# A planner's smaller TensorE grant for background work in each step, and another place where the attention sums' tile is allocated

## The chip, the cores and the metric

The kernel runs on one core of a Trainium2 chip. The metric is device time in microseconds of one execution; the time of a kernel is the median of its runs. Engine names in the profile: PE is TensorE's matmuls and PEld its weight loads, DVE is VectorE, ACT is ScalarE, POOL is GpSimd, SP is SyncE, which here only issues DMAs.

## The reference

Input x is 8 images of 256 channels by 32 x 32 pixels, all in float32. Two layers follow each other.

Layer 0 normalises x in groups of channels and adds an attention over the image:

```
q = q_w . x                                  8 heads of 32, 1024 queries
k_map, v_map = kv_w . x                      256 channels each
pooled(t): for sides 32, 16, 11, 5: average-pool t, add its 3x3 depthwise convolution
k, v = layernorm(pooled(k_map)), layernorm(pooled(v_map))     1426 keys
att = softmax(q . k / sqrt(32)) . v
out = proj_w . (att mixed within each head) + proj_b
x = x + out
```

Layer 1 takes the 1024 pixels of an image as tokens: layer norm, an attention over 256 channels with one head, then a layer norm and a mixture of eight dense experts of three matrices each, weighted by a gate that is a softmax over the mean of all images. Both parts are added to their input.

## The kernel before, in words

**A planner writes the order.** No engine decides at run time what to do next. While the program is built, the class `Flow` (line 665) keeps a modelled clock for every engine (`now`), and for every tile the modelled time at which it is written and read (`ready`, `read`). Each instruction goes through `note` (line 786), which prices it with `cost` (line 744), advances the engine's clock, and ties it behind the last instruction of its engine. The order in which the builder emits instructions is thus the order in which each engine runs them.

**Foreground.** `attention` (line 954) walks through a list of 360 steps (`steps`, line 2124): for each of 8 images b, for the two channel halves c (four heads each), for two halves of the queries (512), for eleven chunks of 128 keys; one more step for each image computes the scores of the last 25 keys of all four combinations together ("tail", at the ninth place of the image). A step emits `scores` (line 1650): four matmuls of 32 rows in a tile sc of four PSUM banks, of which there is one, and ScalarE's exponential into a tile pt. Then, for the chunk of the step before, `values` (line 1660): four matmuls of 32 columns that accumulate into pv. After the last chunk of a combination, `tail_values` adds the tail's part, and ScalarE copies pv to the tile att (line 2177), which is allocated once for each (b, c) (line 2144) in one of two buffers.

**Background.** All other work is written as generators, called threads, that yield what they need next: an engine, the tiles that have to be there, and a PSUM tag. `spawn` sorts them by rank. Rank 0: the sums of the probabilities (`unit`, `sums`), the normalisation, the reading back of queries. Rank 1: `project` (line 1767), which multiplies att by a matrix in four chunks and adds the result in DRAM, with a buffer xr between; also the pooling by halves (`halve`) and the start of the small convolutions. Rank 2: `value_tokens` and `key_tokens`, which transpose the convolved maps by groups of four and layer-norm them. Rank 4: `prepare` (line 1500), the next image's load, its statistics, the four maps (`maps`, line 1227, three chunks each: 512, 512 and 146 pixels) and its queries (`queries`, line 1549, four chunks, written to DRAM and read back). The convolution's taps on VectorE (`convolve`, line 1394) have rank 7. Layer 1 has ranks 5 and 6 (`outputs`, `layer1`, `norm`). I call the work of ranks 0 to 4 preparation for short, and the TensorE work between two yields of a thread a chunk.

**How much of it goes between two steps.** After each step the loop calls `f.step((PACE, PACE1))` (line 2179). `step` (line 923) adds PACE = 4.0 us of planned TensorE time to the credit of ranks under 5 and PACE1 = 2.0 to that of ranks from 5 up (`FILLER`), each held to 1.5 times its pace (`CAP`), and then resumes threads in the order of rank as long as one is runnable; what a thread spends on TensorE is taken from its credit (line 921), which can go below zero. For TensorE a thread is runnable (lines 902 to 911) when its inputs are planned to be there 1.5 us before `until`, a PSUM buffer is free by then, and

```
until = max(pe, self.free("sc") - 0.5)
(self.credit[rank >= FILLER] > 0 or pe < until - 0.5)
```

that is, when there is credit, or when TensorE's modelled clock pe is over 0.5 us before the time at which sc comes free for the next scores. The call in the middle of a step (line 2155), without a pace, is closed to TensorE.

**Due times.** `finish` (line 936) is the other way in which threads run: the loop calls it where it can't go on without something, and it resumes whichever thread can start first, with the credit set to 1.0, until the condition holds. The places are the key tokens of the image (line 2140, before chunks 0, 4 and 8, and line 2150 before the tail), its queries (line 2142), a free pt (line 2153), the value tokens (line 2164), and at the end of a combination the projection of the image before (line 2176). The maps run ahead within limits: `maps` waits for free map buffers and for earlier maps to be convolved, and an image's fourth map needs the value tokens of that image, which wait for the image before it to be in attention.

**After the loop** the rest of layer 1 runs down, and `experts` (line 2323) fills TensorE to the end; parts of it start while layer 1 still runs.

All operations of `Flow` are recorded at line 678, so the profile's groups are told apart by tiles: sc and pv are the foreground; kvw marks maps, qw queries, mt the projection, con with acc, sacc or kt the transposes of tokens, pt with con the sums; y, p, v, t, gw, wv, res and diag belong to layer 1; bank and y with t, h and s3e to the experts.

Of the kernel before, what the change touches and what calls it, by code (L numbers as in the profile page):

```python
# [16 lines left out]
P = 128  # L17
C = 256
HW = 1024
# [9 lines left out]
SCALE0 = DH ** -0.5  # L29
SCALE1 = C ** -0.5  # L30
FILLER = 5
PACE = 4.0
PACE1 = 2.0
CAP = (1.5, 1.5)
NEVER = 1e9
# [918 lines left out]
def attention(tc, kit, f, outer, ended, nb, consts, x, t1, t2, hn, bounds, vecs, q_t, kv_t, proj_t, gqk_t, wqk, wqkv, vecs1, w1_d, w1c, gate_d, wrc, vecs2, bnvec, w2_d, h2d, between, pre, held):  # L954
# [6 lines left out]
    with ExitStack() as ctx:  # L961
        l1, shared = outer
        wp = ctx.enter_context(tc.tile_pool(name="w0", bufs=1))
        work = ctx.enter_context(tc.tile_pool(name="work0", bufs=1))
        psum = ctx.enter_context(tc.tile_pool(name="psum0", bufs=1, space=PSUM))

        def T(pool, shape, tag, bufs=1):
            return f.tile(pool, shape, tag, bufs=bufs)
# [681 lines left out]
        def scores(b, c, sl, kc):  # L1650
            k0, w = KEY_CHUNKS[kc]
            t = T(psum, [P, 4, 512], "sc")
            for j in range(4):
                r = slice(DH * j, DH * j + DH)
                f.pe.matmul(t[:w, j, :], lhsT=ks[b, c][r, k0 : k0 + w], rhs=qs[b, c][r, sl], start=True, stop=True)
            pt = T(work, [P, 4, 512], "pt", bufs=6)
            f.act.activation(pt[:w], t[:w], AF.Exp, scale=SCALE0)
            return pt

        def values(b, c, kc, pt, pv):  # L1660
            w = KEY_CHUNKS[kc][1]
            for j in range(4):
                h = 4 * c + j
                f.pe.matmul(
                    pv[DH * j : DH * j + DH, :],
                    lhsT=vts[b][kc // 4][:w, kc % 4, h * DH : (h + 1) * DH],
                    rhs=pt[:w, j, :],
                    start=kc == 0,
                    stop=False,
                )  # L1670

        def tail_scores(b):
            t = T(psum, [P, 4, 512], "sc")
            for j in range(4):
                r = slice(DH * j, DH * j + DH)
                for u in range(4):
                    c, half = divmod(u, 2)
                    f.pe.matmul(
                        t[DH * u : DH * u + DH, j, :],
                        lhsT=ks[b, c][r, NK - DH :],  # L1680
                        rhs=qs[b, c][r, half * 512 : half * 512 + 512],
                        start=True,
                        stop=True,
                    )
            f.act.activation(ptail, t, AF.Exp, scale=SCALE0)

        def tail_values(b, u, pv):
            for j in range(4):
                f.pe.matmul(
                    pv[DH * j : DH * j + DH, :],  # L1690
                    lhsT=vz[b % 2][DH * u : DH * u + DH, DH * j : DH * j + DH],
                    rhs=ptail[DH * u : DH * u + DH, j, :],
                    start=False,
                    stop=True,
                )

        def tail_add(u, into):
            rows = slice(DH * (u + 1) - NT, DH * (u + 1))
            f.pool.dma_start(
                out=into[:NT].rearrange("p j q -> p (j q)"),  # L1700
                in_=ptail[rows].rearrange("p j q -> p (j q)"),
                accum_op=ALU.add,
            )

        def add(kc, pt, into):

            w = KEY_CHUNKS[kc][1]
            f.pool.dma_start(
                out=into[:w].rearrange("p j q -> p (j q)"), in_=pt[:w].rearrange("p j q -> p (j q)"), accum_op=ALU.add
            )  # L1710
# [120 lines left out]
        projected, taken, written, probabilities = [0], [0], [0], []  # L1831
# [276 lines left out]
        def unit(b, c, sl, n, pairs):  # L2108
            total = yield from sums(n, pairs)
            yield from normalise(b, c, sl, total, n)  # L2110

        atts = {}
# [22 lines left out]
        for i in range(len(steps) + 1):  # L2135
            if i < len(steps):
                b, c, half, kc = steps[i]
                sl = slice(half * 512, half * 512 + 512)
                if kc % 4 == 0:
                    f.finish(lambda: key_parts[0] > 3 * b + kc // 4)  # L2140
                if (half, kc) == (0, 0):
                    f.finish(lambda: (b, c) in qs and (b or (c, 0) in asked))
                    turn[0] = 2 * b + c
                    atts[b, c] = T(work, [P, HW], "att", bufs=2)
                if kc == NKC // 2 and b < nb - 1:
                    f.sp.dma_start(t1[b][:, c, sl], x[b, c * P : (c + 1) * P, sl])
                if b == 0 and kc == 0:
                    f.finish(lambda: (c, half) in asked)
                if kc == NKC - 1:
                    f.finish(lambda: key_parts[0] > 3 * b + 2 and (b, 1) in qs and (b or len(asked) == 4))  # L2150
                    tail_scores(b)
                else:
                    f.finish(lambda: f.vacant("pt"))
                    pts[i] = scores(b, c, sl, kc)
                f.step()
            if i and steps[i - 1][3] < NKC - 1:
                b1, c1, half1, kc1 = steps[i - 1]
                if kc1 == 0:
                    pv = T(psum, [P, 512], "pv")
                    pairs = []  # L2160
                    sl1 = slice(half1 * 512, half1 * 512 + 512)
                    f.spawn(unit(b1, c1, sl1, units, pairs), 0)
                    units += 1
                f.finish(lambda: kc1 // 4 in vts[b1])
                values(b1, c1, kc1, pts[i - 1], pv)
                spent[0] += kc1 == 3
                if kc1 % 2:
                    f.drop(pts[i - 1])
                    add(kc1, pts.pop(i - 1), pts[i - 2])
                    pairs.append(pts.pop(i - 2))  # L2170
                if kc1 == NKC - 2:
                    u = 2 * c1 + half1
                    tail_values(b1, u, pv)
                    pairs.append(pts.pop(i - 1))
                    tail_add(u, pairs[-1])
                    f.finish(lambda: projected[0] >= b1)
                    f.act.activation(atts[b1, c1][:, sl1], pv, AF.Copy)
            if i < len(steps):
                f.step((PACE, PACE1))
        f.columns, f.keep = False, None  # L2180
# [536 lines left out]
def tile_conv_attn_hybrid(  # L2717
# [45 lines left out]
    with tc.tile_pool(name="between", bufs=1) as between, ExitStack() as early:  # L2763
        l1 = early.enter_context(tc.tile_pool(name="l1", bufs=1, side="right"))
        shared = early.enter_context(tc.tile_pool(name="psum_l1", bufs=1, space=PSUM, side="right"))
        f = Flow(tc, kit)

        ended, pre, held = [0], set(), {"w": {}, "todo": []}
        attention(
            tc, kit, f, (l1, shared), ended, nb,  # L2770
            consts, x, t1, t2, hn, bounds, vecs0, q_t, kv_t, proj_t, gqk_t, wqk, wqkv, vecs1, w1_d, w1c, gate_d, wrc, vecs2, bnvec,
            w2_d, h2d, between, pre, held,
        )
        last(f, (l1, shared), ended, early, pre, held)
# [122 lines left out]
```

## Time and profile before

| | us |
|---|---|
| median of three runs | 3174.4 (3173.14 to 3174.69) |
| the profiled execution | 3177.97 |
| its span, first to last instruction | 3176.1 |
| attention loop, by the first scores and the last | 83 to 1825 |
| rest of layer 1 and experts | 1825 to 3176 |

The profile's first part gives each engine's busy time, its share of the span and the number of its instructions. A table by window gives, after the window's limits and length, the busy time of PE, PEld, DVE, ACT and POOL with their instruction counts, then the granted TensorE clock as a share of full speed, the busy share of the DMA engines and the GB/s moved. A list of waits gives who waited for whom, the sum, the number of times and the longest. The timeline gives start, length, engine, operation, tiles, shapes and the number of merged instructions, and in brackets the idle time ahead of it with what ended it. A matmul's length is modelled: the next may start before it is over, so chunks are best measured from start to start. Matmuls of float32 appear twice as often as they are written, and a wide one in four column tiles four times that.

### The profile page before, as it was taken

How to read it: one execution, taken by the hardware profiler on the slowest of the kernel's cores; microseconds unless marked ns; L12 is line 12 of the kernel's file. 1: busy time of each engine (PE TensorE's matmuls, PEld its weight loads, DVE VectorE, ACT ScalarE, POOL GpSimd, SP SyncE). 2: the span in 40 equal slices, each digit the busy share in tenths (PEclk: the TensorE clock that was granted, in tenths of full speed). 3: DMA queues.
4: the chain of work that ended last, by engine and by line, in shares of the span. 5: the costliest groups of instructions: out<-in, count | busy, mean ns of one | idle time of the engine just before them, and what ended most of it. 6: DMA issues, size and time to landing. Idle time of an engine off the chain costs nothing.

```text
span 3176.1 us, 56426 instructions
## 1 busy us (share of the span) xinstructions
PE 3052.5 (96%) x22778; PEld 1794.2 (56%) x22778; DVE 2284.5 (72%) x3823; ACT 1627.8 (51%) x2175; POOL 1287.8 (41%) x1387
## 2 busy tenths in 40 slices
PE   7898899999999999989999999999999999999998
PEld 3332233434434334434433376768888888888887
DVE  6865785995887877877444444558888877777776
ACT  3766666566576576675565523343333344444443
POOL 3423241332332332331221202038566667777776
PEclk9899999999999999999999999999999999999999
DMA  1366855766666666666776725244344310000000
GB/s 55 80 155 142 183 107 116 174 132 128 155 138 138 138 140 142 143 146 134 180 149 131 179 68 202 91 164 148 139 144 149 108 39 21 22 32 21 21 14 22
DMA packets 114223, 364.40 MB, mean 115 GB/s; under 512 B 13904, under 2 KB 40056, under 8 KB 90496
## 3 DMA queue, kind: packets, MB, share of 16 engines
q0 software_dynamic: 28608, 181.68, 29.5%
q1 hardware_dynamic: 81840, 177.02, 16.6%
q8 instruction: 182, 2.98, 0.4%
q10 hardware_dynamic: 3504, 1.99, 0.2%
q14 instruction: 89, 0.73, 0.1%
HBM read 112.99 MB, written 80.26 MB: 61 GB/s over the span
## 4 chain that ended last, share of the span: by engine, by line
PE 70%; DVE 8%; issue 3%; ACT 3%; DMA 3%; POOL 2%; SPq 0%; DVEq 0%; POOLq 0%; ACTq 0%
PE bank L678 21%; PE sm L678 16%; PE y L678 10%; PE sc L678 8%; PE sx L678 7%; PE pv L678 7%; DVE acc L678 2%; ACT pt L678 2%; DMA pt<-pt 2%; DVE pt L678 1%; DVE h L678 1%; DVE u L678 1%; DVE c L678 1%; DMA xi<-in_x_dram 1%; ACT h L678 0%
## 5 line engine op out<-in xcount | busy, mean ns | idle before, releaser
L678 ACT ACTIVATE pt<-sc 128x2048 f32<-128x2048 f32 (+1 forms) x352 | 660.6, 1877 | 310.7 <-PE sc L678 257.0
L678 PE MATMUL sc<-q,kn 32*128 32x512 f32 (+2 forms) x3072 | 417.9, 649 | 49.4 <-ACT pt L678 48.2
L678 DVE TENSOR_TENSOR pt<-pt,pt 128x1024 f32<-128x1024 f32 x280 | 340.6, 1261 | 113.9 <-DMA pt<-pt 111.1
L678 PE MATMUL pv<-pt,vt 128*32 128x512 f32 (+1 forms) x2816 | 379.4, 611 | 0.2 <-ACT att L678 0.2
L678 ACT ACTIVATE h<-h,bnvec 128x512 f32<-128x512 f32 x454 | 343.4, 805 | 65.8 <-DVE h L678 55.6
L678 ACT ACTIVATE p1c<-bank 128x256 f32<-128x256 f32 x227 | 86.8, 382 | 559.0 <-PE bank L678 553.1
L678 DVE SCALAR_TENSOR_TENSOR acc<-map,vec,acc 128x961 f32<-128x961 f32 (+1 forms) x240 | 316.4, 1322 | 31.3 <-ACT acc L678 25.5
L678 POOL TENSOR_TENSOR rstd<-rstd,mhalf 128x4 f32<-128x4 f32 (+2 forms) x88 | 109.9, 1250 | 560.4 <-DVE rstd L678 470.2
L678 POOL DMA_DIRECT2D pt<-pt x160 | 147.1, 920 | 405.0 <-ACT pt L678 319.6
L678 DVE TENSOR_TENSOR h<-p1c,bank 128x512 f32<-128x512 f32 x227 | 154.7, 682 | 201.6 <-PE bank L678 198.5
L678 POOL TENSOR_TENSOR tm<-h,tm 128x256 f32<-128x256 f32 x212 | 242.8, 1145 | 16.6
L678 PEld LDWEIGHTS sc<-q,kn 32*128 32x128 f32 (+2 forms) x3072 | 113.0, 178 | 224.0 <-ACT pt L678 118.8
L678 DVE TENSOR_TENSOR h<-u,bank 128x256 f32<-128x256 f32 x454 | 231.3, 550 | 7.8
L678 POOL TENSOR_TENSOR tm<-h 128x512 f32<-128x512 f32 x106 | 140.1, 1321 | 200.1 <-ACT h L678 198.0
L678 PEld LDWEIGHTS pv<-pt,vt 128*32 128x32 f32 (+1 forms) x2816 | 55.8, 108 | 272.2 <-issue 259.7
L678 DVE SCALAR_TENSOR_TENSOR sacc<-small,vec,sacc 128x480 f32<-128x480 f32 (+8 forms) x384 | 194.8, 515 | 14.9 <-ACT sacc L678 4.7
L678 DVE TENSOR_TENSOR h<-h,gate 128x1024 f32<-128x1024 f32 x128 | 202.4, 1581 | 0.5 <-ACT h L678 0.5
L678 PE MATMUL y<-t,s3e 128*128 128x256 f32 x768 | 187.0, 379 | 3.1 <-POOL t L678 1.8
L678 POOL TENSOR_TENSOR t<-h,t 128x256 f32<-128x256 f32 x218 | 173.8, 797 | 17.1
L678 POOL TENSOR_TENSOR t<-h 128x512 f32<-128x512 f32 x109 | 141.4, 1297 | 94.8 <-DVE h L678 74.1
L678 PE MATMUL bank<-t,s1e 128*128 128x256 f32 x726 | 177.6, 381 | 0.0
L678 DVE TENSOR_TENSOR u<-h,bank 128x512 f32<-128x512 f32 x227 | 156.1, 688 | 25.1 <-PE bank L678 0.8
(374 smaller groups left out, 5663.0 us busy)
## 6 DMA issues: line engine op xcount, KB each, us to landing
pt<-pt POOLq DMA_DIRECT2D x160, 1024.0 KB, 7.8
h<-h SPq DMA_DIRECT2D x111, 512.0 KB
xi<-in_x_dram SPq DMA_DIRECT2D x16, 512.0 KB
t<-t SPq DMA_DIRECT2D x8, 1024.0 KB
res<-t SPq DMA_DIRECT2D x32, 256.0 KB
t<-res SPq DMA_DIRECT2D x32, 256.0 KB
hn<-res SPq DMA_DIRECT2D x32, 256.0 KB
hn<-hn SPq DMA_DIRECT2D x16, 512.0 KB
```

The lines of the kernel that those rows point to most:

```text
L678: ins = fn(*args, **kwargs)
```

## The change

Two things. The grant of ranks under 5 goes from 4.0 to 1.2 us a step (its upper limit from 6.0 to 1.8 with it); the grant of layer 1 stays. And the tile of the sums is allocated just before it is first written, at the end of a combination's first half, where it was allocated at the start of the half of the heads, eleven steps earlier; the `finish` for the projection of the image before moves ahead of it, and so ahead of the tail's values and its addition.

```diff
-PACE = 4.0
+PACE = 1.2
 PACE1 = 2.0
 CAP = (1.5, 1.5)
...
                 if (half, kc) == (0, 0):
                     f.finish(lambda: (b, c) in qs and (b or (c, 0) in asked))
                     turn[0] = 2 * b + c
-                    atts[b, c] = T(work, [P, HW], "att", bufs=2)
...
                 if kc1 == NKC - 2:
+                    f.finish(lambda: projected[0] >= b1)
+                    if half1 == 0:
+                        atts[b1, c1] = T(work, [P, HW], "att", bufs=2)
                     u = 2 * c1 + half1
                     tail_values(b1, u, pv)
                     pairs.append(pts.pop(i - 1))
                     tail_add(u, pairs[-1])
-                    f.finish(lambda: projected[0] >= b1)
                     f.act.activation(atts[b1, c1][:, sl1], pv, AF.Copy)
```

## The prediction

> **What bounds the kernel now.** I read the page's busy shares first, then the busy times by window with the windows cut where each image's attention begins, then the list of waits for TensorE, and last TensorE's timeline at two places.
>
> ```profile
> PE 3052.5 (96%) x22778; PEld 1794.2 (56%) x22778; DVE 2284.5 (72%) x3823; ACT 1627.8 (51%) x2175; POOL 1287.8 (41%) x1387
> ```
>
> TensorE is busy 96% of the span. No other engine is near it, so time is TensorE's work plus its gaps, and a change of order can win back gaps only.
>
> ```profile
> 83.00:308.00 225.00, 200.48 (x1736) 72.06 (x1736) 163.94 (x325) 153.78 (x200) 79.23 (x96) 0.95 0.56 125
> 308.00:517.00 209.00, 193.40 (x1878) 71.87 (x1882) 156.03 (x265) 136.33 (x162) 64.61 (x74) 0.98 0.67 144
> ...
> 1193.00:1405.00 212.00, 202.56 (x1916) 83.00 (x1912) 175.75 (x314) 138.24 (x165) 67.19 (x80) 1.00 0.70 150
> ...
> 1625.00:1825.00 200.00, 197.77 (x2210) 73.23 (x2206) 91.22 (x151) 110.97 (x99) 36.39 (x40) 1.00 0.71 150
> 1825.00:3176.00 1351.00, 1328.68 (x5908) 1111.04 (x5904) 970.61 (x1445) 493.08 (x814) 759.32 (x761) 1.00 0.24 83
> ```
>
> The second number is the window's length, the third TensorE's busy time. The eight attention windows (83 to 1825 us) leave 81 us idle in all: 24.5 in the first image, 15.6 in the second, 12.0, 5.7, 8.4, 9.4, 3.8 and 2.2 after that. The diff touches only this stretch; what follows 1825 us is TensorE-bound at 98% and only shifts.
>
> ```profile
> PE sc L678 <- ACT pt L678: 48.2, 63, 3.0
> PE sm L678 <- DVE mv L678: 15.8, 2, 10.3
> ```
>
> 48.2 us in 63 waits: the scores of a step (sc) wait for ScalarE's exponential of the step before (pt), since sc has one buffer. By window it is 15.0, 6.8, 5.4, 4.9, 3.8, 8.1, 2.1 and 2.0. Of the other row 10.3 us lie before the loop.
>
> ```profile
> 1122.79 1.06 PE L678 MATMUL pv<-pt,vt 128*32 128x512 f32 x8
> 1123.67 1.90 PE L678 MATMUL sm<-xi,kvw 128*32 128x512 f32 x16
> 1125.39 1.90 PE L678 MATMUL sx<-xi,kvw 128*32 128x512 f32 x16
> 1127.11 0.68 PE L678 MATMUL sm<-xl,kvw 128*32 128x146 f32 x16
> 1127.61 1.90 PE L678 MATMUL sm<-xi,kvw 128*32 128x512 f32 x16
> 1129.32 1.90 PE L678 MATMUL sx<-xi,kvw 128*32 128x512 f32 x16
> 1131.15 1.14 PE L678 MATMUL sc<-q,kn 32*128 32x512 f32 x8
> ```
>
> ```profile
> 1370.31 1.14 PE L678 MATMUL sc<-q,kn 32*128 32x512 f32 x8
> 1371.38 1.06 PE L678 MATMUL pv<-pt,vt 128*32 128x512 f32 x8
> 1373.45 1.14 PE L678 MATMUL sc<-q,kn 32*128 32x512 f32 x8 [1.00 <-ACT pt L678]
> 1374.52 1.06 PE L678 MATMUL pv<-pt,vt 128*32 128x512 f32 x8
> 1376.64 1.14 PE L678 MATMUL sc<-q,kn 32*128 32x512 f32 x8 [1.05 <-ACT pt L678]
> ```
>
> The first is a burst: five chunks of the next image's preparation inside one step (9.4 us from scores to scores). The second is starved: scores, values, nothing else, and about 1.05 us of waiting. A step has a floor of 3.14 us, set by ScalarE, of which TensorE's own part is 2.07; with one chunk (1.72 us, start to start) it is 3.79 with no wait. So a step wants at least 1.07 us of other work. Bursts spend in one step what later steps lack.
>
> **What the Trainium skill says.** "TensorE: Matmul & The Clock Gate", Part 2 (step by step): matmuls stay in program order, only weight loads are pulled ahead. So the order the planner writes down is the order that runs; the trace agrees where TensorE waits 1.05 us with more chunks a few steps on. The same page, Part 1: the clock falls after an idle window of about 3.4 us. The trace grants 0.95 in the first image, where waits are most, and 1.00 in the windows from 1193 us. "TensorEngine Tiling (Array Packing)", Key Properties: changing the tiling mode drains the engine. The trace agrees: from values (128x32 tiles) to a chunk in the same tiles is 0.88 us (1122.79 to 1123.67), to untiled transposes 0.99 us elsewhere.
>
> **The change, part by part.**
>
> *PACE 4.0 to 1.2.* In each step the threads of ranks 0 to 4 (sums, projection, tokens, maps, queries) get 1.2 us of planned TensorE time instead of 4.0, at most 1.8 in hand instead of 6.0. No instruction is added or removed. What they need: from the timeline, sorted by tiles and summed start to start, they take 72 us in the first image, 48 in the second, 43 to 44 in each of the next four: about 0.96 us a step over 45 steps. In the planner's own prices (lines 753 to 758 and 813) an ordinary image is 15.8 for maps, 6.9 queries, 6.9 projection, 3.5 sums, 12.8 for eighteen groups of transposes with their mode switch, 0.8 statistics: 46.7, or 1.04 a step against 1.2. So the grant holds the mean. It isn't a hard limit either: line 908 lets a thread run without credit while the planner sees TensorE free over 0.5 us ahead of `until`. After the values of an ordinary step the planner stands about 1.0 us past the scores' end and `until` (line 904: sc free at 0.15 + 1.87 + 0.15, less 0.5) at 1.67, so one chunk goes in whatever the credit. Preparation then runs at one large chunk, or one to two small ones, per step, where it had up to four or five.
>
> What that wins: bursts of 5.5 to 8.3 us come once or twice an image. Spread at one chunk a step, each reaches four to six steps on. Starved steps lie there in part: after the burst at 1339 us come nine waits between 1364 and 1397, six of them of about a microsecond, of which the spread reaches the first two or three. By image: in the first, 15.0 us of waits less two single long ones (3.0 and 2.8) leaves 9, and the work at hand is plentiful; I take two thirds, **6 us**. In the second to sixth, 6.8 + 5.4 + 4.9 + 3.8 + 8.1 = 29.0; I take a third, **10 us**. In the last two, nothing. Ends for this part: 0, if what is spread meets only full steps, and 38 (all of the 9 and the 29).
>
> What it costs: transposes that shared a step fall in separate ones; each extra change of tiling costs 0.11 us in and about as much out; ten more make **2 us** (0 to 8). The layer-1 threads (ranks 5 up) keep 2.0 a step, one chunk of 1.72, so their rate per step stands; if the freed slot goes to preparation first they lose at most the second chunk that some steps have, and it is done after 1825 us at the same price.
>
> What is late next: maps come up to six steps later, and VectorE's convolution with them. In the fifth image the last key tokens were transposed at 913 us and are due at the tail step, 1021: 108 us spare, or over 20 steps. Queries of the second image were written at 218 us and are due at 308: 90 us, 18 steps; there the first image's 72 us against a grant of 55 leaves 17 us, 14 steps' worth, so it just holds. DMAs that move: query writes (256 KB) and the next image's load behind them on SP, whose queue already waits 311.6 us for the query tiles; nothing on SP waits longer for the loop than those 18 steps allow. On POOL the halving (1.28 us a piece) comes between the additions of pt in smaller lots, which is no loss: 0.
>
> *The sums' tile allocated at evacuation, and `finish` moved ahead of the tail's values.* The tile has two buffers; its first write already came after the projection of the last image, by line 2176. Allocation issues no instruction: 0. `finish` emits something only when the projection is late. In the fifth image the projection's four chunks ran between 985 and 1013 us, in the fifth to ninth step, and the check comes at the twelfth; rank 1 keeps them near one a step. If late, TensorE would have the remaining chunks ahead of the tail's values (1.06 us), and behind those wait the copy of the sums on ScalarE and POOL's tail addition; each chunk waits for its buffer's write, 4.8 us to land. Ends: 0 to 20 us an image; I take 0.
>
> **Sum.** 6 + 10 - 2 = 14 us. The profiled execution took 3178.0 us (span 3176.1 and 1.9 around it), so 3164.0 for it; it lies 3.6 above the median 3174.4, which gives 3160.
>
> **Rivals.**
> A, the forecast: part of the starved steps filled, 8 to 24 us won, 3150 to 3166, likeliest 3160. Chance 0.50.
> B, preparation becomes a steady background that is at hand in nearly every starved step: 30 of the 38 us, and 4 to 6 us more from the clock in the first image (5% of 225 us is 11, half of it): 3140. For it: 45 steps and 40-odd chunks an image. Against: the convolution gates the maps, so preparation is not always at hand. Chance 0.17.
> C, the change doesn't do what it says: the rule of line 908 gave one chunk a step before and gives it now, gates of VectorE decide when chunks come; 3174. For it: many steps before had no preparation although credit was 4.0. Against: the bursts are there. Chance 0.13.
> D, slower: preparation falls behind its due step, and `finish` (lines 2140 to 2150) forces it while scores stand. Its price is the missing convolution: eight taps of 1.32 us for a map, 10.6 us, at each of four or five image starts, 42 to 53 us, less half of the 14 won and some of the wait covered by layer 1: about +16, 3190. It decides once preparation is over 18 steps late in the second image or 20 later. For it: the first image needs 1.57 us a step and gets 1.2, unused credit over 1.8 is lost, and the debt carries on. Against: the free chunk, and 90 to 108 us of slack. Chance 0.20.
>
> **Numbers.** A measurement of this kernel can tell about 0.2% (6.3 us) from no change. A falls below 3168 nearly always; faster 0.66 (A 0.49, B 0.17), same 0.14, slower 0.20. The range for 8 in 10 leaves out half of B below and half of D above: 3140 to 3188.
>
> **What would show it.** Right: the waits of sc for pt fall from 48.2 us to 30 to 36; steps with four map chunks are gone; the 98% stretch begins 10 to 20 us earlier than 1825 and keeps its length of 1351. D would show as waits over 5 us for VectorE (acc, kt, sacc) or for q at an image's start. C would show the same bursts. The prediction is wrong if the gain comes from after 1825, or if more than ten such waits stand in the loop.

## The result, and the profile after

The changed kernel took 3157.28 us (median of four runs, 3155.23 to 3158.89), against 3174.55 us for the kernel before (3173.14 to 3176.05): a ratio of 0.9945, 95% interval 0.9928 to 0.9962, or 17 us less. The profiled execution took 3158.89 us, with a span of 3157.0 against 3176.1.

The busy line of the page after:

```profile
PE 3054.6 (97%) x22768; PEld 1796.5 (57%) x22768; DVE 2277.6 (72%) x3824; ACT 1630.0 (52%) x2176; POOL 1286.5 (41%) x1393
```

TensorE's work is what it was (3052.5 before, +2.1), so the whole gain shows as idle time of TensorE: 3176.1 - 3052.5 = 123.6 us before, 3157.0 - 3054.6 = 102.4 after, 21.2 less. 21.2 - 2.1 = 19.1 is the difference of the two spans. Where this idle time was is seen when each trace is cut at its last scores. Limits, length and TensorE's busy time, then clock, DMA share and GB/s; first the kernel before:

```profile
83.00:1817.66 1734.66, 1652.95 (x16602) 0.99 0.66 142
1817.66:3176.10 1358.44, 1336.02 (x6004) 1.00 0.24 84
```

and after:

```profile
83.00:1808.84 1725.84, 1664.63 (x16656) 0.99 0.66 142
1808.84:3157.00 1348.16, 1326.62 (x5944) 1.00 0.24 82
```

The loop's idle time goes from 1734.66 - 1652.95 = 81.7 us to 61.2, that is 20.5 of the 21.2. The stretch after it idles 22.4 and 21.5. Yet the loop is only 8.9 us shorter, and the stretch after it 10.2: in the loop TensorE was busy 11.7 us longer, with 54 matmuls more, and after it 9.4 us less, with 60 fewer. Layer-1 work moved from the end into the loop. So a gap won back in the loop shows up partly as an earlier end of the loop, partly as layer-1 work done earlier. The granted clock was lower as well, 0.989 over the whole profiled execution against 0.991 in the one before, which makes some 6 us more lost at most (an estimate: what is missing to 1, times the span). The 2.3 us that TensorE was busy longer beyond the moved work can be its doing; no run isolates it.

By image, from its first scores to those of the next:

| image | 1 | 2 | 3 | 4 | 5 | 6 | 7 | 8 |
|---|---|---|---|---|---|---|---|---|
| TensorE idle, before | 25.9 | 14.2 | 12.0 | 5.7 | 8.4 | 9.5 | 3.8 | 2.2 |
| after | 19.3 | 10.4 | 4.6 | 10.5 | 5.3 | 2.5 | 7.9 | 0.7 |
| of it sc waiting for pt, before | 15.8 | 6.1 | 5.4 | 4.9 | 3.8 | 8.1 | 2.1 | 2.0 |
| after | 7.8 | 6.1 | 3.1 | 7.0 | 5.1 | 2.1 | 3.7 | 0.6 |

In this count six images win, the fourth and the seventh lose. TensorE's waits in the loop after, with sum, number and longest:

```profile
PE sc L678 <- ACT pt L678: 35.5, 49, 2.8
...
PE sm L678 <- DMA res<-in_w_dram: 4.7, 1, 4.7
PE sx L678 <- DVE acc L678: 3.9, 1, 3.9
```

The scores' waits fell by 48.2 - 35.5 = 12.7 us. The other waits in the loop fell too, by about 8 us; most of them are single ones of up to 5.5 us.

**The bursts are gone.** In the timeline before, the fifth image had five chunks of maps and queries between two scores, at 1122.79 to 1131.15 us. Steps with more than 5 us of preparation, measured start to start, were 13 in the loop before and are 2 after. After, the three chunks of a map lie in three successive steps, with layer-1 products beside them:

```profile
1128.26 1.92 PE L678 MATMUL sm<-xi,kvw 128*32 128x512 f32 x16
1130.01 1.04 PE L678 MATMUL sm<-diag,con 128*32 128x512 f32 x8
1130.98 1.14 PE L678 MATMUL sc<-q,kn 32*128 32x512 f32 x8
1132.05 1.07 PE L678 MATMUL pv<-pt,vt 128*32 128x512 f32 x8
1132.93 1.90 PE L678 MATMUL sx<-xi,kvw 128*32 128x512 f32 x16
1134.65 3.64 PE L678 MATMUL sm<-wv,t 128*32 128x256 f32 x64
1138.21 1.14 PE L678 MATMUL sc<-q,kn 32*128 32x512 f32 x8
1139.28 1.06 PE L678 MATMUL pv<-pt,vt 128*32 128x512 f32 x8
1140.17 0.68 PE L678 MATMUL sx<-xl,kvw 128*32 128x146 f32 x16
```

**A third of the starved steps is gone.** By length alone (scores to scores in under 3.25 us) the short steps are hardly fewer, 59 before and 58 after; but a short step can hold a small chunk. Steps with nothing but scores and values in them, the prediction's sense of starved, are 29 before and 19 after, and waits of about one microsecond before scores (0.9 to 1.15 us) fell from 29 to 15.

The longer of the two heavy steps left is at the twelfth step of the second image, where `finish` now stands ahead of the tail's values:

```profile
341.73 1.90 PE L678 MATMUL sm<-att,mt 128*32 128x512 f32 x16
343.45 1.90 PE L678 MATMUL sx<-xi,kvw 128*32 128x512 f32 x16
345.17 0.68 PE L678 MATMUL sm<-xl,kvw 128*32 128x146 f32 x16
345.67 1.90 PE L678 MATMUL sm<-att,mt 128*32 128x512 f32 x16
347.50 0.33 PE L678 MATMUL sx<-con,acc 128*128 128x128 f32 x1
351.71 0.55 PE L678 MATMUL sx<-con,acc 128*128 128x128 f32 x3 [3.89 <-DVE acc L678]
...
354.85 1.93 PE L678 MATMUL pv<-ptail,vz 32*32 32x512 f32 x8
356.71 2.09 PE L678 MATMUL sc<-q,kn 32*128 32x512 f32 x8
```

Two chunks of the projection (att with mt) were late and stand ahead of the tail's values; `finish` resumes whichever thread can start first, and so two chunks of a map come with them, and transposes that wait 3.89 us for the convolution (acc). Only then come the tail's values and the next scores: the step lasts 16.9 us (339.8 to 356.7).

### The profile page after: what moved, and what is told of

Same layout as the page of the kernel before. It is cut to its first block, busy times and chain, and to the rows that moved or that the text cites. A ratio compares the mean times of both kernels' runs of the same rounds, so it can differ in the third digit from the quotient of the medians.

```text
span 3157.0 us, 56376 instructions
## 1 busy us (share of the span) xinstructions
PE 3054.6 (97%) x22768; PEld 1796.5 (57%) x22768; DVE 2277.6 (72%) x3824; ACT 1630.0 (52%) x2176; POOL 1286.5 (41%) x1393
## 4 chain that ended last, share of the span: by engine, by line
PE 80%; DVE 8%; ACT 4%; issue 4%; DMA 2%; POOL 2%; ACTq 0%; DVEq 0%; POOLq 0%
PE bank L678 22%; PE sm L678 20%; PE y L678 11%; PE sc L678 10%; PE sx L678 9%; PE pv L678 9%; ACT pt L678 3%; DVE acc L678 3%; DMA pt<-pt 2%; DVE h L678 1%; DVE pt L678 1%; DVE u L678 1%; DVE c L678 1%; DMA res<-in_w_dram 1%; ACT h L678 0%
## 5 line engine op out<-in xcount | busy, mean ns | idle before, releaser
L678 PE MATMUL sc<-q,kn 32*128 32x512 f32 (+2 forms) x3072 | 417.9, 645 | 37.1 <-ACT pt L678 35.5
L678 DVE TENSOR_TENSOR pt<-pt,pt 128x1024 f32<-128x1024 f32 x280 | 347.6, 1285 | 137.0 <-DMA pt<-pt 118.5
L678 DVE SCALAR_TENSOR_TENSOR acc<-map,vec,acc 128x961 f32<-128x961 f32 (+1 forms) x240 | 307.4, 1283 | 13.4 <-ACT acc L678 7.8
L678 PE MATMUL sm<-y,t 128*32 128x256 f32 (+1 forms) x2112 | 175.2, 379 | 0.0
```

The costliest lines, as they stand in the source:

```text
L678: ins = fn(*args, **kwargs)
```

## The experiments

All are the changed kernel with one edit. Ratios are to the kernel before, with 95% intervals. The theory at the start: the smaller grant keeps chunks for steps that otherwise lack them, and the second part is worth nothing. Its rivals: the gain is the second part's, or the gain is an accident of the order that the planner happens to write.

**The second part alone.**

```diff
-PACE = 1.2
+PACE = 4.0
```

> Only the second part of the change: the sums' tile at its evacuation and the finish ahead of the tail, the grant still 4.0. Theory 1 (the smaller grant spreads bursts over starved steps, the second part is neutral): 3171 to 3178 us, the scores' wait for the exponential near 48 us, as before. Theory 2 (the later allocation or the earlier finish does it): 3155 to 3162. Theory 3 (any change of order moves the time by some 10 us either way, whatever it is for): anywhere from 3160 to 3190, and the scores' wait doesn't go with the time.

Measured: 3187.7 us, 1.0035 (1.0021 to 1.0049): slower by 13 us than the same grant with the old place. TensorE's order is that of the kernel before, instruction for instruction, until the twelfth step of the second image. There the kernel before has

```profile
365.28 1.06 PE L678 MATMUL pv<-pt,vt 121*32 121x512 f32 x8
366.27 1.06 PE L678 MATMUL pv<-ptail,vz 32*32 32x512 f32 x8
367.26 1.92 PE L678 MATMUL sx<-att,mt 128*32 128x512 f32 x16
369.12 0.65 PE L678 MATMUL sm<-con,kt 128*128 128x128 f32 x4
```

and this one

```profile
363.82 1.07 PE L678 MATMUL pv<-pt,vt 121*32 121x512 f32 x8
364.70 1.90 PE L678 MATMUL sx<-att,mt 128*32 128x512 f32 x16
366.54 0.66 PE L678 MATMUL sm<-con,kt 128*128 128x128 f32 x4
367.13 1.06 PE L678 MATMUL pv<-ptail,vz 32*32 32x512 f32 x8
```

Two chunks changed places with the tail's values. On the spot that cost 0.8 us: this step and the next take 10.36 us here and 9.53 in the kernel before. But from there every modelled clock differs, the planner makes other choices, and at the end the kernel is 13 us slower, with 63.5 us of waits of sc for pt against 48.2. Most of the added waits lie in the rest of this same image: 18.9 us in the second image against 6.1. So at a grant of 4.0 the second part gains nothing, and it can't be the gain by itself; and a difference of 13 us can follow from a displacement that on the spot costs 0.8. That made the third account, accident, a serious one, and the next runs look at the grant at many values.

**The grant at other values**, with the allocation at its new place.

```diff
-PACE = 1.2
+PACE = 2.0
```

> The change with a grant of 2.0 in place of 1.2: up to 3.0 us in hand, so two large chunks in a row are still possible. Theory 1: part of the gain, 3160 to 3168 us, the scores' wait between 36 and 45 us. Theory 3: no order between 4.0, 2.0 and 1.2.

Measured: 3155.24 us, 0.9934 (0.9918 to 0.9949).

```diff
-PACE = 1.2
+PACE = 1.4
```

> The change with a grant of 1.4. Run 1 (second part alone, 13 us slower by moving two chunks once) says that a small change of order can shift the whole plan after it, so single paces scatter by some 10 us; the question is whether the low grants lie together under the high ones. Theory 1 (a small grant wins by spreading): 3150 to 3164 us. Theory 3 (scatter alone): 3155 to 3190, no side taken.

Measured: 3161.03 us, 0.9955 (0.9941 to 0.997).

```diff
-PACE = 1.2
+PACE = 1.6
```

> The change with a grant of 1.6. Theory 1: 3150 to 3166 us, beside 1.2, 1.4 and 2.0. Theory 3: 3155 to 3190, no side taken.

Measured: 3168.99 us, 0.9984 (0.9977 to 0.9991).

```diff
-PACE = 1.2
+PACE = 3.0
```

> The change with a grant of 3.0 (4.5 in hand, bursts of two to three large chunks). The second part emits nothing different at this grant. Theory 1: with the high grants, 3170 to 3190 us, the scores' wait for the exponential above 45 us. Theory 3: 3155 to 3190, no side taken.

Measured: 3197.74 us, 1.0071 (1.0043 to 1.0099).

```diff
-PACE = 1.2
+PACE = 5.0
```

> The change with a grant of 5.0, larger bursts than before. Theory 1: 3172 to 3192 us, the scores' wait 48 us or more. Theory 3: 3155 to 3190, no side taken.

Measured: 3181.45 us, 1.0025 (1.001 to 1.0039).

At 2.0, 3.0 and 5.0 TensorE's order is the same with the allocation at its old place, instruction for instruction, since `finish` then has nothing left to force; so these three are runs of the grant alone. What follows: there is no smooth curve. The four grants from 1.2 to 2.0 took 3155 to 3169 us, their mean is 3160.6; the three from 3.0 to 5.0 took 3181 to 3198, mean 3189.0; the kernel before (4.0 with the old place), 3174.6, is faster than these three. The two groups don't overlap, so the smaller grant is very likely a cause, worth some 28 us between the means at the new place. But inside a group neighbours differ by 4 to 14 us without an order in them, which no account of mine predicts: that is the scatter of the orders. Pure accident is unlikely: of the 35 ways to choose four of the seven kernels, only one puts the four fastest at the four smallest grants. The exact size of 17 us isn't explained by the grant alone.

**The grant under the need.**

```diff
-PACE = 1.2
+PACE = 0.8
```

> The change with a grant of 0.8, under the mean need of 0.96 to 1.04 a step. Theory 1: the free chunk still gives one chunk a step when TensorE would wait, so nothing collapses: 3152 to 3165 us, the scores' wait 30 to 38 us; no forced waits over 5 us at the starts of images. Rival (a grant under the mean makes preparation late and finish forces it): 3175 to 3200, with waits for acc, kt or q.

Measured: 3245.87 us, 1.0219 (1.0202 to 1.0237). The list of waits alone hardly shows why:

```profile
PE sc L678 <- ACT pt L678: 54.6, 56, 3.8
...
PE sc L678 <- DMA q<-hn: 7.0, 1, 7.0
```

The rest is in the groups of TensorE's instructions, among products of a constant with a constant:

```profile
L678 PE MATMUL sm<-con 128*128 128x256 f32 x188 | 41.8, 381 | 0.0
L678 PE MATMUL sx<-con 128*128 128x256 f32 x42 | 9.4, 379 | 0.0
```

These compute nothing that is used: `warm` (line 847) writes such filler wherever the planner sees TensorE wait over 1.8 us, to keep it busy. With others like them in the tiling of the values (128x32) they are 61 us in the loop, 9.0 in the kernel before, and they count as busy. The two groups shown stand mostly at the starts of images, at 295 to 308 us (14 us) and 6 to 7 us each at 754, 999, 1232, 1458 and 1698 us. That is rival D's place and mechanism: preparation comes too late and the next image waits for it. The loop ends at 1914 us, 105 us later than after.

```diff
-PACE = 1.2
+PACE = 1.0
```

> The change with a grant of 1.0, between the change (3157) and 0.8 (3246). The mean need is 0.96 us a step as measured and 1.04 in the planner's prices. If the edge is where the grant no longer covers the need: 3175 to 3215 us, with forced work at the starts of images and filler products. If the free chunk covers a small deficit: 3155 to 3170.

Measured: 3181.85 us, 1.0021 (1.0012 to 1.003). So the edge lies between 1.0 and 1.2. At 1.0 the filler is only 9.7 us; there is one wait for the queries (5.1 us), and the scores' waits are 50.3 us. The longest of these names ScalarE, but ScalarE had stood behind the evacuation of a map, which waited for VectorE's convolution:

```profile
364.66 0.60 ACT L678 ACTIVATE map<-sm 128x512 f32<-128x512 f32 x1 [9.82 <-DVE acc L678]
365.16 0.77 ACT L678 ACTIVATE acc<-sm,vec,mid 128x512 f32<-128x512 f32 x1
365.82 1.88 ACT L678 ACTIVATE pt<-sc 128x2048 f32<-128x2048 f32 x1
```

TensorE's next scores come at 367.75 us, after 7.43 us of waiting. A step of 16.1 us stands shortly before (339.86 to 355.96); in it, late chunks of the projection and chunks of maps stand together before the tail's values. That is late preparation, as rival D has it, though its due point is the projection.

**The free chunk of line 908**, which preparation may run without credit, taken away from it.

```diff
-                and (self.credit[rank >= FILLER] > 0 or pe < until - 0.5)
+                and (self.credit[rank >= FILLER] > 0 or rank >= FILLER and pe < until - 0.5)
```

> The change, but a thread of ranks 0 to 4 no longer runs without credit when TensorE would wait. Theory 1: starved steps with preparation at hand but credit in debt go unfilled, and the first image (1.57 us a step needed, 1.2 granted) falls behind: the scores' wait 48 us or more, 3170 to 3190 us. Rival (the credit alone does the spreading, the free chunk is rarely used): 3154 to 3162, as the change.

Measured: 3182.8 us, 1.0024 (1.0017 to 1.0031), with this wait:

```profile
PE sc L678 <- ACT pt L678: 67.2, 66, 4.8
```

35.5 us with the rule, 67.2 without, and 25.5 us more time, beyond the 4 to 14 by which neighbours differ: at a grant of 1.2 there is no gain without the rule. By the code it is what lets a chunk into an otherwise starved step when the credit is spent; steps with nothing but scores and values are 28 here, 19 with the rule.

**The limit on what may be in hand**, apart from the grant. With 5.0 times 1.2 it is 6.0 us, as it was in the kernel before.

```diff
-CAP = (1.5, 1.5)
+CAP = (5.0, 1.5)
```

> The change with the same mean grant of 1.2, but up to 6.0 us of unused credit in hand (5 times the pace instead of 1.5), as much as before the change. Theory 1a (what counts is that bursts are cut): bursts come back after every stretch in which preparation had no work, 3168 to 3185 us. Theory 1b (what counts is the mean, which keeps preparation spread over the image): 3152 to 3165. Loop idle plus filler products, which went with the time in all runs so far, 70 to 80 us under 1b and 85 to 95 under 1a.

Measured: 3150.57 us, 0.9918 (0.9905 to 0.993), the fastest of the study. Its interval touches that of the change (0.9928 to 0.9962), so it is as fast or a little faster. Some bursts come back in it: seven steps have over 5 us of preparation, against two with the change and 13 before. Yet steps with nothing but scores and values are 16, fewer than with the change. So seven bursts in the loop don't cost the time, against the picture that my prediction had; what counts is the grant per step. Why is argued only: the grant sets how soon after a burst the next chunks follow. Changes of tiling, from the values' tiles to untiled ones, are 95 in this loop against 107.

```diff
-PACE = 1.2
+PACE = 1.0
-CAP = (1.5, 1.5)
+CAP = (5.0, 1.5)
```

> The grant is 1.0 us a step, and 5.0 us may be in hand (1.5 with the limit at 1.5 times the grant, which took 3181.9). Theory L, lost credit: 1.0 is near enough to the mean need (0.96 by the timeline, 1.04 in the planner's prices), and 1.0 failed because what a step left unused beyond 1.5 was lost; with 5.0 in hand nothing is lost, and the time is that of the grant of 1.2, 3148 to 3164, with the waits of sc for pt at 38 to 46 us. Rival theory G, the grant: 1.0 is below what the planner charges, preparation runs late whatever may be in hand, and a wait for the queries or filler products at the images' starts stay: 3174 to 3190.

Measured: 3178.62 us, 1.0013 (1.0006 to 1.002). So lost credit isn't why 1.0 fails, and the grant is, as theory G had it. The change of tiling just counted comes 129 times in this loop, and the scores wait 54.9 us for pt. Of the marks that G named the filler is there (16.9 us in the loop), the wait for the queries isn't.

**How long ahead of the scores a thread must be ready.** If the planner were too careful in letting threads in, a smaller margin would fill more steps.

```diff
-MARGIN = 1.5
+MARGIN = 1.0
```

> The change, and a thread may take TensorE when its inputs are planned to be there 1.0 us ahead, not 1.5. In the order of instructions it leaves about 8 us less room unfilled between values and scores than the change. Theory 1 (time follows the unfilled room of the loop): 3143 to 3153 us, the scores' wait under 32 us. Rival (inputs come later than planned and TensorE waits for them instead): 3155 to 3170, with the scores' wait lower and the other waits higher by as much.

Measured: 3161.07 us, 0.9957 (0.9945 to 0.9969): no gain over the change, against my expectation. The loop's idle time is nearly the same (59.2 us against 61.2). Starved steps are only 11 here, but waits of the scores of over 1.15 us sum to 14.6 us against 9.5.

**One account for all runs.** For each I summed TensorE's gaps in the timeline between 83 us and its last scores (all those before sc, whatever was waited for, and the rest) and the time of the filler in the same stretch:

| kernel | median us | gaps before sc | other gaps | filler | sum | span less sum |
|---|---|---|---|---|---|---|
| limit 5.0 times | 3150.6 | 45.1 | 12.8 | 12.0 | 69.9 | 3078.9 |
| grant 2.0 | 3155.2 | 53.8 | 10.8 | 8.9 | 73.5 | 3081.4 |
| the change (1.2) | 3157.3 | 37.1 | 24.0 | 8.5 | 69.6 | 3087.4 |
| 1.4 | 3161.0 | 46.9 | 17.9 | 15.0 | 79.8 | 3077.1 |
| margin 1.0 | 3161.1 | 40.2 | 18.7 | 6.5 | 65.4 | 3094.4 |
| 1.6 | 3169.0 | 54.6 | 21.1 | 5.4 | 81.1 | 3090.0 |
| before (4.0) | 3174.6 | 49.5 | 32.1 | 9.0 | 90.6 | 3085.5 |
| 1.0, limit 5.0 times | 3178.6 | 56.6 | 16.6 | 16.9 | 90.1 | 3081.5 |
| 5.0 | 3181.5 | 54.0 | 25.0 | 12.4 | 91.4 | 3089.0 |
| 1.0 | 3181.9 | 59.4 | 16.4 | 9.7 | 85.5 | 3094.4 |
| no free chunk | 3182.8 | 70.5 | 12.7 | 6.9 | 90.1 | 3089.3 |
| 4.0, new place | 3187.7 | 66.3 | 20.9 | 10.1 | 97.3 | 3088.9 |
| 3.0 | 3197.7 | 72.3 | 20.6 | 11.0 | 103.9 | 3093.0 |
| 0.8 | 3245.9 | 64.2 | 19.1 | 61.1 | 144.4 | 3107.3 |

Without the last row the spans cover 48 us (3148.8 to 3196.9) and what is left after the sum covers 17 (3077.1 to 3094.4). So most of what tells the kernels apart is idle and filler time in the loop; of the rest, some is the granted clock (below, what stays open). No single column does it: the grant of 2.0 has more waits of sc than the kernel before, and wins by its other gaps; the 0.8 loses by filler.

The count of starved steps (nothing but scores and values) parts them more clearly. It is 11 to 26 in the six kernels up to 3169 us, and 29 to 37 in the kernel before and at 3.0, 4.0 and 5.0. So a grant of 3.0 or more goes with more starved steps, as the prediction had it. A grant of 1.0 or less fails in another way: with 21 to 24 starved steps the two kernels at 1.0 and the one at 0.8 have 20 to 32 us in waits of the scores of over 1.15 us, against 9.5 to 18 in the six.

## Why the prediction was right, and where it wasn't

The time was forecast at 3160 and is 3157.3; rival A's case came true. Point by point:

- **TensorE bound, only gaps to win: held.** Busy +2.1, idle -21.2.
- **Sum of 14 us for the profiled execution: 19.1 measured.** The first image's 6 is 8.0 by the scores' waits (15.8 to 7.8) and 6.6 by all idle time. The 10 us of the second to sixth image were mis-sized as I counted them: the scores' waits there went from 28.3 to 23.4 only, 4.9 won. But the other waits in the same images fell by 11.6 (idle 49.8 to 33.3, less the 4.9), and I had given those no gain at all. The total came out near because one term was too large and one left out; that is luck. The last two images, set at nothing, lost 2.6. If filler is counted as waiting, the place was wrong as well: it was 9.1 us in the first two images before and 1.0 after, and none against 7.4 in the fourth and fifth. Idle time and filler together fell by 18.5 us in the first two images, where my terms hold 8.3 (6, and a third of the second image's 6.8), and by 5.3 in the third to sixth, where they hold 7.4.
- **Two us for ten more changes of tiling: near in number, not shown in time.** They went from 100 to 107 in the loop. TensorE's busy time rose by 2.1, but that can't be put down to them, since the lower granted clock alone is worth some 6 us (the estimate above).
- **Waits of sc for pt to 30 to 36 us: held, 35.5.** Steps with four map chunks: gone. Starved steps went from 29 to 19, near the third that I took. As a cause the burst is weaker than I made it: with the limit at 5.0 times there are seven bursts again, but starved steps are 16 and the time is no worse. What counts is a grant per step between the mean need and twice that (1.2 to 2.0), together with the free chunk (without it 3182.8). The step that isn't borne out is "bursts spend in one step what later steps lack".
- **"Their rate per step stands; keeps its length of 1351": failed.** The stretch after the loop began 8.9 us earlier, not 10 to 20, and was 10.2 us shorter, with 9.4 us less work for TensorE. By my own sign of being wrong, a gain from after the loop, half of the time won counts against me; of the idle time won 20.5 us of 21.2 lie in the loop. I had taken the credit as what holds layer 1 back; line 908 lets it, too, run beyond its credit where a step has room, and steps freed of a burst have. That this is the reason is read from the code; no run isolates it.
- **The second part at 0: failed as a claim, though small on the spot.** `finish` did force chunks in the second image; I had looked at the fifth only. In the changed kernel they cost a step of 16.9 us with 3.9 of waiting in it, inside my bound of 0 to 20. Alone, at 4.0, the second part made the kernel 13 us slower by what followed from it.
- **Rival D: its mechanism is real, its point lies elsewhere.** At 1.2 it doesn't decide: only one wait of 3.9 us for acc, none for q. At 0.8 it does, and at 1.0 in part (the 7.43 us behind the convolution, the 5.1 for the queries). My need of 1.04 in the planner's prices and 0.96 in the trace lie where the edge is, between 1.0 and 1.2; the debt of the first image carried on less than I feared; that the free chunk pays it is argued, not isolated.
- **Rival B's clock: not seen.** The first image was granted 0.93 after, 0.95 before (see the last section).
- **Rival C: out.** The bursts did go, and the grants from 1.2 to 2.0 are all faster than those from 3.0 to 5.0.

What stays open: why one grant inside a group is 4 to 14 us better than its neighbour. The runs show that a displacement of two chunks is enough for 13 us, not by which chain of choices. So of the 17 us the direction is explained by the grant; how much is its mean effect and how much the luck of this order can't be told from one order. The grant of 1.2 with the allocation at its old place was not tried.

A part of the scatter is the granted clock. Of 25 executions of the kernel before, measured together, one with a mean clock of 0.988 took 3181.1 us, and three with 0.994 took 3172.9 to 3173.6. What is missing to 1, times the span, is an estimate of what the clock took at most. On the mean it is 29.2 us for the change, 24.6 to 27.4 for the kernel before, 17.0 for the limit at 5.0 times, and 31.9 for the second part alone. So the gain of the change isn't the clock's. The lead of the limit at 5.0 times over the change (6.7 us) can be, and so can up to 7 of the 13 us that the second part alone lost. Between the groups it is 25.8 us at the four small grants and 30.0 at the three large ones, 4 of the 28 us. Whether a kernel's order or chance sets its clock is not shown.

## What to carry to other kernels

When a planner writes one static order, give background work per step somewhat more than it needs on the mean, and never less: with a need of 0.96 to 1.04 us, grants of 1.2 to 2.0 were the fast ones here, the grant of 1.0 lost the whole gain, and 0.8 cost 2%. Before a change of 10 us in such a planner is believed, run neighbours of the parameter; a single order's time carries 4 to 14 us of luck here, so the mean of a group says what a parameter does and the best member is what one ships. And count filler as waiting: TensorE's busy share was 96% both in the kernel before and in the one that was 2% slower.

## What was not expected of the hardware

The granted clock of the first image fell although TensorE idled less there. Limits, length, busy time, clock, before and then after:

```profile
82.90:311.50 228.60, 202.71 (x1753) 0.95 0.57 125
```

```profile
83.40:296.40 213.00, 193.66 (x1567) 0.93 0.62 138
```

Idle time is 25.9 and 19.3 us. The whole difference lies in the first 18 us, before and then after:

```profile
82.90:101.00 18.10, 14.57 (x95) 0.84 0.18 38
```

```profile
83.40:101.00 17.60, 15.92 (x84) 0.63 0.29 76
```

What is missing to 1, times the length, is 2.9 us before and 6.5 after, and for the whole image 11.4 and 14.9. But up to 104 us TensorE's order is the same in both kernels. So what differs there is not the smaller grant's doing. At 94.10 us before, values took 1.06 us; at 95.53 us after, where the clock is 0.50, they took 1.94. The scores' waits for pt in this stretch are 2.2 us before and 1.7 after, so a small part of the first image's smaller idle time can come from slower products. The Trainium skill has the clock fall after an idle window of about 3.4 us ("TensorE: Matmul & The Clock Gate", Part 1). The trace agrees at 284 to 291 us after, where the clock is 0.51 at the end of a wait of 4.7 us (res from a DMA). In the first 18 us it doesn't show this: no wait there is longer than 1.4 us.

And a releaser can stand for another. The longest of the 49 waits of sc for pt, 2.85 us at 1115.28, names ScalarE, whose row there is

```profile
1113.35 1.88 ACT L678 ACTIVATE pt<-sc 128x2048 f32<-128x2048 f32 x1 [5.28 <-DMA pt<-pt]
```

ScalarE itself waited 5.28 us for a transfer that adds one pt to another and so frees the buffer. TensorE's 2.85 us of waiting had 3.20 us of filler ahead of it in the same step, at 1109.23.
